# Five places for x instead of three: longer load stretches and whole-slot stores in a store-bound pairwise product kernel

## The chip, the cores and the metric

The kernel runs on one core of one Trainium2 chip. The metric is the device time of one execution in microseconds (us), the median of several executions. "The trace" is one execution taken by the hardware profiler.

## The reference, cut to what matters

```python
def _L0_rec_ref(x, W):                       # x: (4096, 32, 64) f32, W: (64, 64) f32
    vid = jnp.einsum('bfd,de->bfe', x, W)
    idx_i, idx_j = jnp.triu_indices(32, k=1) # 496 pairs of fields, i < j
    return x[:, idx_i, :] * vid[:, idx_j, :] # (4096, 496, 64) f32
```

The input is 33.6 MB and the output 520.1 MB. Almost all of the time goes into writing the output.

## The kernel before: the parts that matter

The batch is cut into 16 tiles of x, each of 128 partitions x 32 fields x 128 numbers, 2.097 MB. TensorE makes `vid` from a tile, in the on-chip memory PSUM. VectorE multiplies x by `vid` for the 496 pairs and writes the products into a slot in the on-chip memory SBUF. A slot goes to DRAM in one or more stores; one pair is 65,536 B. All loads and stores are issued by the SyncE sequencer (SP) on one queue, in the order of the program.

```python
SLOT = 116                                   # pairs in a slot, three slots
GROWING = [45, 46, 25, 55, 61, 44, 72, ...]  # small stores in the first ten slots (cut)
xpool = ctx.enter_context(tc.tile_pool(name="x", bufs=3))
opool = ctx.enter_context(tc.tile_pool(name="out", bufs=3))
...
    load(4)                                  # first tile, in four pieces
    load()
    load()
    for t in range(NT):
        xt = loaded[t]
        ...                                  # 16 matmuls into vid
        for at, m, w, i, di, j, dj in products(blocks(t), t * NP):
            ...                              # one tensor_tensor per block of pairs
            nc.vector.tensor_tensor(o, left, right, ALU.mult)
            at += n
            if at == until or at in (base + SLOT, NT * NP):
                nc.sync.dma_start(out=out[:, sent:at, :], in_=ot[:, sent - base : at - base, :])
                ...
        if t % 2:
            load()
            load()
```

`blocks(t)` takes the pairs of the first two tiles field by field (the first products need few fields) and those of the others in square blocks (fewer, larger operations).

Of the kernel before, what the change touches and what calls it, by code (L numbers as in the profile page):

```python
# [1 line left out]

# [4 lines left out]

F32 = mybir.dt.float32
ALU = mybir.AluOpType

P = 128

C = 128

SLOT = 116

GROWING = [
    45, 46, 25, 55, 61, 44, 72, 58, 58, 77, 39, 87, 29, 76, 40, 90, 26, 33,
    83, 84, 32,
]  # L20

XPAD = 8
OPAD = 24


def by_field():

    return [("row", j, 0, 1, j) for j in range(1, 32)]


def by_block():


    def within(lo):
        yield "step", lo, 2, 1, 0
        for k in range(2):
            yield "step", lo, 4, 2, k
        for i in (lo, lo + 8):
            yield "row", i + 4, i, 4, 4
        yield "row", lo + 8, lo, 8, 8  # L40

    yield from within(0)
    yield "row", 16, 0, 16, 16
    yield from within(16)


def blocks(t):
    return by_field() if t < 2 else by_block()


def products(blocks, at=0):

    for kind, a, b, c, d in blocks:
        if kind == "row":
            rows, n, i0, di, j0, dj = c, d, b, 0, a, 1
        else:
            rows, n, i0, di, j0, dj = 16 // b, c, a, b, a + c + d, b
        r = k = 0
        while r < rows:
            room = SLOT - at % SLOT  # L60
            if k or room < n:
                m, w = 1, min(n - k, room)
            else:
                m, w = min(rows - r, room // n), n
            yield at, m, w, i0 + r * di + k, di, j0 + r * dj, dj
            at += m * w
            if k + w == n:
                r, k = r + m, 0
            else:
                k += w  # L70


def pairs(blocks):

    for _, m, w, i, di, j, dj in products(blocks):
        for r in range(m):
            for k in range(w):
                yield i + r * di + k, j + r * dj


@with_exitstack
def pairwise_bilinear_kernel(
    ctx: ExitStack,
    tc: tile.TileContext,
    x: bass.AP,
    w: bass.AP,
    out: bass.AP,
):




    nc = tc.nc
    NT = x.shape[0]
    F = x.shape[2] - XPAD
    D = P // 2
    NP = F * (F - 1) // 2

    BANK = 512 // C


    ctx.enter_context(tc.manual_schedule(engines={mybir.EngineType.SP}))

    const = ctx.enter_context(tc.tile_pool(name="const", bufs=1))
    xpool = ctx.enter_context(tc.tile_pool(name="x", bufs=3))
    opool = ctx.enter_context(tc.tile_pool(name="out", bufs=3))
    psum = ctx.enter_context(
        tc.tile_pool(name="ps", bufs=1, space=bass.MemoryType.PSUM)
    )
    vid = psum.tile([P, F, C], F32)  # L110


    w2 = const.tile([P, D], F32)
    nc.sync.dma_start(out=w2, in_=w)  # L114

    loaded = []

    def load(pieces=1):
        t = len(loaded)
        if t == NT:  # L120
            return
        xt = xpool.tile([P, F, C], F32, tag="x", name=f"x_{t}")
        n = F // pieces
        for lo in range(0, F, n):
            nc.sync.dma_start(out=xt[:, lo : lo + n, :], in_=x[t][:, lo : lo + n, :])
        loaded.append(xt)

    load(4)
    load()
    load()  # L130

    growing = iter(GROWING)
    until = next(growing)
    sent = 0
    for t in range(NT):
        xt = loaded[t]


        for b in range(0, F, BANK):
            for h in range(2):  # L140
                half = slice(h * D, (h + 1) * D)
                nc.tensor.matmul(  # L142
                    vid[half, b : b + BANK, :],
                    lhsT=w2[half, :],
                    rhs=xt[half, b : b + BANK, :],
                    start=True,
                    stop=True,
                )

        for at, m, w, i, di, j, dj in products(blocks(t), t * NP):  # L150
            base = at - at % SLOT
            if at == base:
                ot = opool.tile([P, SLOT, C], F32, tag="o", name=f"o_{at}")
            n = m * w
            o = ot[:, at - base : at - base + n, :]
            if m == 1:
                left = xt[:, i : i + w, :]
                right = vid[:, j : j + 1, :].to_broadcast([P, w, C])
            else:
                o = o.rearrange("p (m w) c -> p m w c", m=m)  # L160
                right = vid[:, j : j + (m - 1) * dj + 1 : dj, :].unsqueeze(2).to_broadcast([P, m, w, C])
                if di == 0:
                    left = xt[:, i : i + w, :].unsqueeze(1).to_broadcast([P, m, w, C])
                else:
                    left = xt.rearrange("p (m d) c -> p m d c", d=di)[:, i // di : i // di + m, i % di : i % di + w, :]
            nc.vector.tensor_tensor(o, left, right, ALU.mult)  # L166
            at += n
            if at == until or at in (base + SLOT, NT * NP):
                nc.sync.dma_start(
                    out=out[:, sent:at, :],  # L170
                    in_=ot[:, sent - base : at - base, :],
                )
                sent = at
                if at == until:
                    until += next(growing, NT * NP)


        if t % 2:
            load()
            load()  # L180


_INS = ["r_x", "L0_rec_W"]
_OUTS = [((4096, 496, 64), "float32")]


# [37 lines left out]
```

## Time and profile before

| | before |
|---|---|
| time, median | 1292.53 us (3 runs), later 1292.44 (6 runs) |
| span of the profiled execution | 1290.5 us |
| moved through the DMA engines | 553.7 MB, mean 429 GB/s |
| VectorE busy | 1087.0 us, 84% |
| TensorE busy | 219.7 us, 17% |
| loads of x after the head | 13, as six pairs and a single one |

How to read it: the 16 DMA engines are busy in every slice of the span, and VectorE waits for stores, not stores for VectorE. The lines for this are in the prediction below. A word on terms used from here on. A *stretch* is a run of loads with no store between them. A *turn* is the place where the queue goes from stores to loads and back to stores; each stretch has one. The *spread* of a transfer is the time between the first and the last of its 16 landings, one for each DMA engine. From the trace's records of landings I take each transfer's *loss*: the time from the last landing of the transfer before it to its own last landing, less what its bytes need at 435.2 GB/s (the ceiling that the prediction cites).

### The profile page before, as it was taken

The numbers are of one execution on the slowest core, as the hardware profiler recorded it, in microseconds if no ns is written. First come the engines' busy times: TensorE is split into PE (matmuls) and PEld (weight loads), VectorE is DVE, ScalarE is ACT, GpSimd is POOL, SyncE is SP. The second block draws the span as 40 slices with busy tenths as digits, with TensorE's granted clock in tenths as the row PEclk, the third lists the DMA queues.
The fourth block names the chain that finished last, engine by engine and source line by source line (L and its number), as shares of the span: only waits on it lengthen the run. The fifth ranks groups of instructions, "written<-read, shape, count | busy, mean of one in ns | idle before, by whom it ended". The sixth has DMA issues, their size and how long they took to land.

```text
span 1290.5 us, 1722 instructions
## 1 busy us (share of the span) xinstructions
PE 219.7 (17%) x512; PEld 44.3 (3%) x512; DVE 1087.0 (84%) x363; POOL 0.2 (0%) x4
## 2 busy tenths in 40 slices
PE   4121112111121111311123111131101311202000
PEld 1000000000000000000000000000000000000000
DVE  7999989999689886889959989689895998979970
POOL 0000000000000000000000000000000000000000
PEclk8555555555555556555555555555556555555555
DMA  9999999999999999999999999999999999999998
GB/s 390 439 429 436 428 414 434 440 433 431 437 426 434 442 418 442 420 442 438 426 433 425 436 439 421 442 426 436 436 421 438 436 425 439 428 436 436 438 426 350
DMA packets 14265, 553.79 MB, mean 429 GB/s; under 512 B 1712, under 2 KB 1712, under 8 KB 2224
## 3 DMA queue, kind: packets, MB, share of 16 engines
q1 hardware_dynamic: 14256, 553.69, 99.6%
q8 instruction: 4, 0.07, 0.0%
q14 instruction: 5, 0.04, 0.0%
HBM read 33.59 MB, written 520.09 MB: 429 GB/s over the span
## 4 chain that ended last, share of the span: by engine, by line
DMA 62%; DVE 34%; issue 2%; PE 0%; DVEq 0%; SPq 0%
DMA out_dram<-o 61%; DVE o L166 34%; DMA x<-in_r_x_dram 0%; PE vid L142 0%; DVEq L166 0%; SPq L114 0%
## 5 line engine op out<-in xcount | busy, mean ns | idle before, releaser
L166 DVE TENSOR_TENSOR o<-x,vid 128x1024 f32<-128x1024 f32 (+18 forms) x363 | 1087.0, 3064 | 166.5 <-DMA out_dram<-o 156.7
L142 PE MATMUL vid<-x,w 64*64 64x512 f32 x512 | 219.7, 990 | 961.1 <-DVE o L166 755.6
L142 PEld LDWEIGHTS vid<-x,w 64*64 64x64 f32 x512 | 44.3, 199 | 1134.8 <-DVE o L166 871.6
L194 POOL MEMSET const-bfloat16-1.0<- 128x1 bf16 x1 | 0.1, 101 | 0.0
L194 POOL MEMSET const-uint8-127<- 128x1 uint8 x1 | 0.1, 101 | 0.0
L194 POOL MEMSET const-float32-0.0<- 128x1 f32 x1 | 0.1, 98 | 0.2 <-issue 0.2
L194 POOL MEMSET const-float32-1.0<- 128x1 f32 x1 | 0.1, 98 | 0.0
## 6 DMA issues: line engine op xcount, KB each, us to landing
out_dram<-o SPq DMA_DIRECT2D x59, 7424.0 KB, 36.7
x<-in_r_x_dram SPq DMA_DIRECT2D x15, 2048.0 KB, 40.7
out_dram<-o SPq DMA_DIRECT2D x2, 3712.0 KB, 16.7
out_dram<-o SPq DMA_DIRECT2D x1, 5760.0 KB, 22.9
out_dram<-o SPq DMA_DIRECT2D x1, 5568.0 KB, 19.4
out_dram<-o SPq DMA_DIRECT2D x1, 5312.0 KB, 37.0
out_dram<-o SPq DMA_DIRECT2D x1, 4928.0 KB, 17.8
out_dram<-o SPq DMA_DIRECT2D x1, 4864.0 KB, 20.9
```

The lines of the kernel that those rows point to most:

```text
L142: nc.tensor.matmul(vid[half, b : b + BANK, :], lhsT=w2[half, :], rhs=xt[half, b : b + BANK, :], start=True, stop=True,)
L166: nc.vector.tensor_tensor(o, left, right, ALU.mult)
L194: nc = _bacc.Bacc("TRN2", target_bir_lowering=False, num_devices=1, dynamic_dma_scratch_size=1024)
```

## The change

The intent of the change is to turn less often between loads and stores: five places for x allow five tiles at the head and then four loads in one stretch, three times (4, 4 and 3). The longer head also gives VectorE the time to fill a whole slot, so the growing stores and the order by fields can go. Five places take room from the slots, which shrink from 116 to 95 pairs.

```diff
-SLOT = 116
-GROWING = [45, 46, 25, ... ]          (cut)
+SLOT = 95
+PLACES = 5
...
-def by_field(): ...                   (cut)
-def blocks(t):
-    return by_field() if t < 2 else by_block()
...
-    xpool = ctx.enter_context(tc.tile_pool(name="x", bufs=3))
+    xpool = ctx.enter_context(tc.tile_pool(name="x", bufs=PLACES))
...
     load(4)
-    load()
-    load()
+    for _ in range(PLACES - 1):
+        load()
...
-        for at, m, w, i, di, j, dj in products(blocks(t), t * NP):
+        for at, m, w, i, di, j, dj in products(by_block(), t * NP):
...
-            if at == until or at in (base + SLOT, NT * NP):
+            if at in (base + SLOT, NT * NP):
                 nc.sync.dma_start(
-                    out=out[:, sent:at, :],
-                    in_=ot[:, sent - base : at - base, :],
+                    out=out[:, base:at, :], in_=ot[:, : at - base, :]
                 )
...
-        if t % 2:
-            load()
-            load()
+        if (t + 1) % (PLACES - 1) == 0:
+            for _ in range(PLACES - 1):
+                load()
```

More of the change, by code (lines that the diff above doesn't have):

```diff
@@ L13 @@
 C = 128
-SLOT = 116
-GROWING = [
-    45, 46, 25, 55, 61, 44, 72, 58, 58, 77, 39, 87, 29, 76, 40, 90, 26, 33,
-    83, 84, 32,
-]
+SLOT = 95
+PLACES = 5
 XPAD = 8
 OPAD = 24
-def by_field():
-    return [("row", j, 0, 1, j) for j in range(1, 32)]
 def by_block():
@@ L128, in pairwise_bilinear_kernel @@
     load(4)
-    load()
-    load()
-    growing = iter(GROWING)
-    until = next(growing)
-    sent = 0
+    for _ in range(PLACES - 1):
+        load()
     for t in range(NT):
@@ L167, in pairwise_bilinear_kernel @@
             at += n
-            if at == until or at in (base + SLOT, NT * NP):
+            if at in (base + SLOT, NT * NP):
                 nc.sync.dma_start(
-                    out=out[:, sent:at, :],
-                    in_=ot[:, sent - base : at - base, :],
-                )
-                sent = at
-                if at == until:
-                    until += next(growing, NT * NP)
-        if t % 2:
-            load()
-            load()
+                    out=out[:, base:at, :], in_=ot[:, : at - base, :]
+                )
+        if (t + 1) % (PLACES - 1) == 0:
+            for _ in range(PLACES - 1):
+                load()
 _INS = ["r_x", "L0_rec_W"]
@@ L220 @@
     for t in range(NT):
-        order = [place[p] for p in pairs(blocks(t))]
+        order = [place[p] for p in pairs(by_block())]
         res[:, t][:, :, order] = got[:, :, t].transpose(0, 3, 2, 1)
```

## The prediction

> **What bounds the kernel now.** I read the page first (slices, bytes, the chain's shares), then the groups, then the chain in order of time, then busy times by stretches for both ends. The page:
>
> ```profile
> DMA  9999999999999999999999999999999999999998
> GB/s 390 439 429 436 428 414 434 440 433 431 437 426 434 442 418 442 420 442 438 426 433 425 436 439 421 442 426 436 436 421 438 436 425 439 428 436 436 438 426 350
> HBM read 33.59 MB, written 520.09 MB: 429 GB/s over the span
> DMA 62%; DVE 34%; issue 2%; PE 0%; DVEq 0%; SPq 0%
> ```
>
> The DMA engines are busy in every slice. Bytes are fixed: 16 tiles of x of 2.097 MB in, 7936 pairs of 65,536 B out. The multiplies are the only other large row:
>
> ```profile
> L166 DVE TENSOR_TENSOR o<-x,vid 128x1024 f32<-128x1024 f32 (+18 forms) x363 | 1087.0, 3064 | 166.5 <-DMA out_dram<-o 156.7
> ```
>
> VectorE is busy 84% of the span and idles mainly for a free slot, that is for a store. So it is ahead, and its time only matters where it might leave the queue empty. The chain in order of time (start, duration, what), where the end of each DMA piece is the landing of a store:
>
> ```profile
> 257.78 36.65 DMA out_dram<-o
> ...
> 310.63 46.65 DMA out_dram<-o
> ...
> 425.67 37.14 DMA out_dram<-o
> ...
> 478.75 47.36 DMA out_dram<-o
> ...
> 1047.40 36.59 DMA out_dram<-o
> ...
> 1100.06 41.35 DMA out_dram<-o
> ...
> 1157.24 36.69 DMA out_dram<-o
> ```
>
> These landings lie three slots apart. From 1141.41 (1100.06 + 41.35) to 1193.93 is 52.52 us for 3 x 116 x 65,536 B = 22.81 MB: 434 GB/s, the rate with stores alone. From 294.43 to 357.28 is 62.85, and from 462.81 to 526.11 is 63.30: a pair of loads between the stores costs 10.35 and 10.8 us, where its 4.19 MB at 434 GB/s need 9.66. From 1083.99 to 1141.41 is 57.42: the one load at the end costs 4.90 against 4.83. So a pair loses 0.7 to 1.1 us, a single load almost nothing.
>
> What that is I looked up in the trace's own records, each DMA's 16 landings and each packet. Five full pairs from the second on lose about 0.6, 1.1, 1.0, 0.9 and 0.9 us, nearly all in the pair's **last** load (the first loses 0.00 to 0.07); the pair at 141 us loses 2.6. In the pair that lands at 654 and 659 us every load packet takes 0.61 us, on into the second load, until other engines begin to store; then some twenty packets take 0.7 to 1.6 us. The loss thus sits at the turn from loads to stores, on the engines still loading. The 16 landings of one transfer spread 1.1 us at the head, 5.3 us at the end: the laggards set the time.
>
> The ends:
>
> ```profile
> 0.00:10.00 10.00, 4.46 (x12) 1.55 (x14) 1.82 (x5) 0.20 (x4) 1.00 0.79 300
> 10.00:20.00 10.00, 8.20 (x36) 2.38 (x32) 10.00 (x9) 0.00 (x0) 1.00 1.03 439
> 1270.00:1280.00 10.00, 0.00 (x0) 0.00 (x0) 0.00 (x0) 0.00 (x0) 0.50 0.94 406
> 1280.00:1290.50 10.50, 0.00 (x0) 0.00 (x0) 0.00 (x0) 0.00 (x0) 0.50 0.43 185
> ```
>
> The last column is GB/s. The first 10 us lose (434 - 300) x 10 = 1.34 MB, 3.1 us; from 10 us on the rate is full, so the growing small stores already hide the head.
>
> Budget: 553.7 MB at 434.4 GB/s is 1274.6 us; the span is 1290.5. Of the 15.9 us between, the start takes 3 to 4, load turns some 7 (2.6 + 4.5 + 0.1), the last receipts and the rest of the spread 4 to 5.
>
> **What the Trainium skill says.** "DMA: Bandwidth & Descriptors", section "Where 436 GB/s comes from", gives a ceiling of 435.2 GB/s at the SBUF ports: stores here run at 434, within 0.3%, so no slot size can speed a store up. The same page, "Rules for kernel authors", asks for at least 1 MiB per DMA; all whole slots and tiles, before and after, exceed that. "VectorE: DVE Perf Modes", section "The TRN2 errata", gives (N+151)/0.96 ns for an fp32 add of two tensors: 1224 ns at N = 1024. With one operand in PSUM the groups here show 1215 (1024), 8681 (8192) and 12948 (12288), which is (N+142)/0.96; I use that. I know no sentence there on a cost of turning from loads to stores; that rests on this trace alone.
>
> **The change, part by part.**
> 1. *Head.* Five tiles are loaded before the first store, not three: the same bytes, moved forward. Nothing is saved if the first store stands in the queue before the loads are through. The third tile landed at 19.25 us; two more at 5.0 each land at 29.2, first engines at about 28, and their data end about a microsecond earlier: the store must be issued by some 25.7 if it needs the 1.3 us that the first small load needed before data flowed. The block order starts with 8 pairs that need fields 0 to 15, thus four PSUM banks: the last matmul of bank 3 ends at 12.0 (11.39 + 0.59). Slot 0 is seven operations: 3 x 1.215 + 2 x 2.281 + 4.415 + 1.081 = 13.7 us, so the store is issued at 25.7. Just in time: 0, at worst some half us of gap. After that a slot takes 13.0 to 14.0 us to multiply (95 x 128 x 1.0417 ns = 12.67, plus 2 to 9 operations at 0.148) against 95 x 65,536 B at 434.4 GB/s = 14.33 us to store: VectorE gains about a microsecond per slot and the queue never runs dry.
> 2. *By fields to by blocks, smaller slots.* Operations go from 363 to 415 by count of the two programs: 52 x 0.148 = 7.7 us at most, all of it under VectorE's 166 us of idle time: 0 on the path.
> 3. *Stores.* 84 in place of 79. Each store's landing falls about 0.04 us behind the pure rate whatever its size: +0.2 us.
> 4. *Load stretches.* Before: six pairs and a single load after the head. After: 4, 4 and 3. If the loss is at the turn, three turns at 1.1 us plus 0.05 for each of the other eight loads make 3.7; before it was 7.4 in all. Saved: 3.7 us.
> 5. *Room.* Four tiles hold the queue for 4 x 2.097 MB / 434.4 GB/s = 19.3 us, while VectorE fills the slots left and then idles some 20 us. When the first store after the stretch lands, two full slots wait in the queue, 28.7 us of work; less the spread of 6 us, 22 remain for a fill of 13 to 14. No gap. The fourth load waits for its tile's last multiply, 84, 73 or 62 pairs into a slot, at most 12 us after the third is issued, with two stores and three loads queued ahead of it: hidden as well. PE refills vid in 8 us under the 17 us of a tile's first half.
>
> Sum: 1292.53 + 0.2 + 0 to 0.5 - 3.7 = 1289.1 or so; I say 1289.0.
>
> **The rivals.**
> *A: the loss is per load that follows a load.* Then 6 such loads before become 3 + 3 + 2 = 8, and the time stays at 1292.5 to 1294. For it: the second of each pair has the loss and the single last load has none. Against it: the packets are slow only from the moment other engines store, not from the start of the second load.
> *B: a hole in the queue.* With slots 18% smaller, the queue holds less; if a stretch, or the fourth load's wait which also holds back the store behind it, empties the queue by 3 us three times, the time is about 1298. Against: 22 us of stock for 14 of work. For: the spread could grow.
> *C: turns cost nothing like the single load's 0.1 and the spread stays small.* Then all 7 us are won: 1285.5. Against: five pairs of six lost 0.6 to 1.1.
> *D: the extra loads at the head delay everything.* 4.19 MB, 9.7 us, if VectorE were the bound; but the queue is busy throughout, so only the order changes.
>
> **Range and chances.** I give the turn theory about 0.7, A 0.15, B 0.07, C 0.08. The turns vary from 0.1 to 2.6 us each, so three of them spread the result by about 2 us either way: 1286.3 to 1292.4. Two per cent is 25.8 us; all the loss that isn't plain rate is 15.9, so faster by 2% is as good as excluded. Slower by 2% needs a queue empty for 26 us, for which nothing speaks.
>
> **What would show it.** In the chain, landings three slots apart should be 43.0 us without loads (18.68 MB) and 63 to 64 with four (43.0 + 19.3 + 1.1): under 63 is C, about 65.5 is A. VectorE's wait for stores should show three long waits of about 20 us, its operations 415. The first slice should read as before, with the first store issued at 25 to 26 us. DMA must be 9 in every slice; an 8 in a slice with loads is B. I am wrong if the spread grows as much with three stretches as with seven, or if the store rate itself shifts from 434 GB/s with the 48,640 B rows.

## The result, and the profile after

The changed kernel takes 1291.01 us in the median (1290.52 to 1291.07, six runs), the kernel before beside it 1292.44 (1292.04 to 1292.58). The ratio is 0.9989, with a 95% interval from 0.9976 to 1.0002. A second set of five runs (e9 below) gave 1290.57 against 1292.41, ratio 0.9987, interval 0.9973 to 1.0000. Ratios are the mean time of one kernel's fast runs over that of the other's fast runs of the same rounds, so they are not quite the ratio of the medians. At 2% the two are the same. The gain is 1.4 to 1.8 us, seen twice with the same sign, but each interval alone still reaches 1. Run by run it is clearer: all 11 runs of the changed kernel (1290.12 to 1291.28) are faster than every run of the kernel before (1291.34 and up).

The page of the changed kernel, busy share of DMA and GB/s in 40 slices, the bytes, the chain's shares and the VectorE row:

```profile
DMA  9999999999999999999999999999999999999998
GB/s 397 435 435 433 433 435 435 432 435 413 432 435 435 435 431 433 432 435 435 419 427 435 435 435 434 435 433 433 433 422 425 433 435 435 434 435 435 435 435 362
HBM read 33.59 MB, written 520.09 MB: 430 GB/s over the span
DMA 58%; DVE 34%; another core or an unknown queue 4%; DVEq 1%; issue 1%; PE 0%; SPq 0%
L151 DVE TENSOR_TENSOR o<-x,vid 128x1024 f32<-128x1024 f32 (+17 forms) x415 | 1092.0, 2698 | 166.2 <-DMA out_dram<-o 155.0
```

The queue never runs dry. There are 415 multiplies as counted, VectorE's 1092 us are 5 more than before and its idle time is the same 166 us, so nothing on VectorE shows in the time. In the GB/s row the three stretches can be seen in the slices with 413, with 419 and 427, and with 422 and 425; elsewhere, but for the two ends, the row stands at 431 to 435.

The waits of the changed kernel (in total, how often, longest): the longest wait of VectorE for a store is now 22.6 us, the first stretch of four loads seen from VectorE. The other two stretches give 22.0 and 17.6, so there are the three long waits that the prediction named.

```profile
DVE o L151 <- DMA out_dram<-o: 155.0, 76, 22.6
```

The chain in order of time (start, duration, what). A piece ends with the landing of a store; the piece called an unknown queue ends, by its time, with a store's landing too.

```profile
287.13 29.79 DMA out_dram<-o
...
330.03 22.52 another core or an unknown queue
...
394.54 29.78 DMA out_dram<-o
...
437.39 29.96 DMA out_dram<-o
...
610.64 29.70 DMA out_dram<-o
...
653.38 21.88 another core or an unknown queue
```

From 424.32 (394.54 + 29.78) to 467.35 lie three slots without loads: 43.03 us for 18.68 MB, again 434 GB/s, so the smaller rows haven't changed the store rate. From 316.92 to 352.55 lie one slot and four loads: 35.63 us, where 6.23 MB and 8.39 MB at 434 GB/s need 33.66. This turn loses 2.0 us. The next one, from 640.34 to 675.26, loses 1.3.

The ends and the first turn in stretches (the last three columns are the granted clock, DMA share and GB/s):

```profile
0.00:10.00 10.00, 4.50 (x12) 1.53 (x14) 0.00 (x0) 0.20 (x4) 1.00 0.81 308
10.00:20.00 10.00, 6.72 (x30) 1.75 (x26) 8.83 (x6) 0.00 (x0) 0.99 1.00 429
20.00:30.00 10.00, 3.94 (x8) 0.59 (x8) 10.00 (x5) 0.00 (x0) 0.50 1.09 451
...
318.00:332.00 14.00, 5.85 (x16) 1.79 (x16) 12.03 (x3) 0.00 (x0) 0.62 1.01 432
332.00:335.00 3.00, 0.00 (x0) 0.00 (x0) 0.00 (x0) 0.00 (x0) 0.50 1.04 328
1270.00:1280.00 10.00, 0.00 (x0) 0.00 (x0) 0.00 (x0) 0.00 (x0) 0.50 0.98 424
1280.00:1290.00 10.00, 0.00 (x0) 0.00 (x0) 0.00 (x0) 0.00 (x0) 0.50 0.41 178
```

The head shows no hole: 429 and 451 GB/s from 10 to 30 us. In the stretch the loads run at 432 GB/s until the last three microseconds before the stores begin, and there at 328 with the engines just as busy. The records of packets say the same in single transfers. From 318 to 332 us a load packet takes 0.61 us; of the 38 that start from 333 to 335 us, 32 take 0.7 to 1.4 us; the first packet of the next store starts at 335.5. At the other side of the stretch the last store packets before the loads take up to 2.63 us (at 313 us) where 1.80 is usual. So a turn costs at both of its sides, and the slow load packets come before the stores begin, not beside them. The prediction read this otherwise ("until other engines begin to store"); but in the pair it names, too, 11 of the 22 slow load packets start before the first store packet, which starts at 655.00 us.

Where the time went, from the landings of both traces, in us. "Loads after the head" counts the stores on both sides of each stretch too. "Jumps" are single store landings away from any load that lose more than 0.15 us at once (up to 1.0 here).

| loss against 435.2 GB/s | before | changed | e9 (changed again) |
|---|---|---|---|
| start, head loads and first store | 4.8 | 5.2 | 5.1 |
| loads after the head, with the stores on both sides | 7.9 | 5.3 | 4.7 |
| jumps | 2.2 | 1.9 | 1.7 |
| all other stores | 2.4 | 2.8 | 3.4 |
| sum at the last landing | 17.3 | 15.3 | 14.9 |
| spread of the last store | 6.1 | 3.9 | 3.6 |
| average landing of the last store, us | 1285.5 | 1284.9 | 1284.8 |

The last two rows were the surprise. The average engine finishes only 0.5 us earlier in the changed kernel. The slowest engine, which sets the time, finishes 2.0 us earlier. Three quarters of the gain is thus a smaller lag of the slowest engine behind the average. Within a turn the average is hit as well: of the 5.3 us of the three stretches the average of the 16 landings loses 4.4.

### The profile page after: what moved, and what is told of

The parts are those of the page before. It is cut to its first block, busy times and chain, and to the rows that moved or that the text cites. A ratio compares the mean times of both kernels' runs of the same rounds, so it can differ in the third digit from the quotient of the medians.

```text
span 1288.7 us, 1786 instructions
## 1 busy us (share of the span) xinstructions
PE 226.6 (18%) x512; PEld 41.9 (3%) x512; DVE 1092.0 (85%) x415; POOL 0.2 (0%) x4
## 4 chain that ended last, share of the span: by engine, by line
DMA 58%; DVE 34%; another core or an unknown queue 4%; DVEq 1%; issue 1%; PE 0%; SPq 0%
DMA out_dram<-o 58%; DVE o L151 34%; DVEq L193 1%; PE vid L127 0%; DMA x<-in_r_x_dram 0%; DVEq L151 0%; SPq L102 0%
## 5 line engine op out<-in xcount | busy, mean ns | idle before, releaser
L151 DVE TENSOR_TENSOR o<-x,vid 128x1024 f32<-128x1024 f32 (+17 forms) x415 | 1092.0, 2698 | 166.2 <-DMA out_dram<-o 155.0
L127 PE MATMUL vid<-x,w 64*64 64x512 f32 x512 | 226.6, 1008 | 959.0 <-DVE o L151 892.6
```

The source lines that it names most:

```text
L127: nc.tensor.matmul(vid[half, b : b + BANK, :], lhsT=w2[half, :], rhs=xt[half, b : b + BANK, :], start=True, stop=True,)
```

## The experiments

The theory after the result: each turn makes the late engines later, by about a microsecond, whatever the length of the stretch, so that the time depends on the number of turns (turn theory). Rivals: the loss goes with the loads that follow another load (length theory); a turn costs more while all engines turn together (spread theory). Each experiment is an edit of the changed kernel. All but e4 gave correct results. The kernel before, run beside them on the same chip, had medians of 1292.36 (e1 to e4), 1292.32 (e5 to e8) and 1292.41 (e9, e10).

**e1: pairs of loads**

```diff
-        if (t + 1) % (PLACES - 1) == 0:
-            for _ in range(PLACES - 1):
+        if (t + 1) % 2 == 0:
+            for _ in range(2):
                 load()
```

> The changed kernel, but its 11 later loads go two after every second tile (2,2,2,2,2,1) in place of 4,4,3; head, slots and stores as in the changed kernel. In the changed kernel's trace the three stretches cost 2.0, 1.3 and 1.8 us over their bytes (5.2 in all), not the 3.7 predicted. Turn theory (each turn from loads to stores costs about 1.2 us, whatever the length of the stretch): six turns, about 7 us, so +2 us on the changed kernel, 1292.5 to 1293.5. Length theory (the loss grows with the loads that follow a load: 5 here against 8): 3 us, so 1289. Spread theory (a turn costs more while all engines turn together): between, falling from turn to turn.

Measured: 1293.16 us (1292.54 to 1293.35), ratio to before 1.0004 (0.9990 to 1.0018). This is 2.2 us above the changed kernel and inside the range of the turn theory. The length theory said 1289. No run of it is as fast as any run of the changed kernel. Loads after the head lose 8.3 us, against 5.3. It also says something of the rest of the change: with six turns to the seven of before, the kernel is not faster than before, so the other parts together (order of the blocks, whole slots, slot size, head) gain nothing, and the longer stretches make the gain.

**e2: single loads**

```diff
-        if (t + 1) % (PLACES - 1) == 0:
-            for _ in range(PLACES - 1):
-                load()
+        load()
```

> The changed kernel, but one load after every tile (eleven stretches of one). Turn theory: eleven turns at about 1.2 us make 13 against 5.2, so about 1299. Length theory (a load alone costs only its bytes, as the single one at the end of the kernel before did, 0.1 us): 1 us against 5.2, so about 1287, which would beat both kernels. Each load should show in the trace as 4.83 us plus its loss.

Measured: 1298.68 us (1296.58 to 1299.46), ratio 1.0045 (1.0032 to 1.0058). The turn theory gave 1299, the length theory 1287. Loads lose 15.8 us in all, 1.4 for each turn. The single load at the end of the kernel before, which cost 0.1, was thus not typical of single loads. The turns also grow dearer as the spread grows: the first five lose 0.4 to 1.3 us, with a spread of up to 4 us in the store before them, the last five 1.8 to 2.0, with 7 to 13 us. That is the opposite of the spread theory. The landings of the last store show where it goes: its average is 1285.9, only 1.0 us later than in the changed kernel, while its last engine is 9.0 us later. The spread has grown to 13.0 us.

**e3: three tiles at the head**

```diff
     load(4)
-    for _ in range(PLACES - 1):
+    for _ in range(2):
         load()
 ...
                 nc.sync.dma_start(out=out[:, base:at, :], in_=ot[:, : at - base, :])
+                if base == 0:
+                    load()
+                    load()
```

> The changed kernel, but only three tiles are loaded at the head, the other two right behind the first store. The first store is issued at about 24.4 us as before, while three tiles are through at about 18. If the five tiles at the head are what fills the time until the first whole slot, the DMA engines stand still for 24.4 + 1.3 - 18 = 7 to 8 us and the time is about 1298.5. If the head doesn't matter because the order of the same bytes is all that changes, it stays at 1291. It also adds one turn (1 us).

Measured: 1299.12 us (1298.16 to 1299.73), ratio 1.0050 (1.0036 to 1.0064), as the head theory expected. Busy time by stretches of this run, to be set against the same two stretches of the changed kernel above (429 and 451 GB/s):

```profile
10.00:20.00 10.00, 7.54 (x30) 1.89 (x26) 8.01 (x6) 0.00 (x0) 1.00 0.76 326
20.00:30.00 10.00, 3.26 (x8) 0.58 (x8) 10.00 (x5) 0.00 (x0) 0.58 0.55 233
```

The DMA engines stand still between the third tile and the first whole slot, while VectorE is busy (10.00 of 10 us in the second line). The first store lands with a loss of 8.9 us. So five tiles at the head do fill the time that the growing stores filled before. (The run also has one turn more than the changed kernel.)

**e4: no loads after the head (wrong result)**

```diff
-        xt = loaded[t]
+        xt = loaded[t % PLACES]
 ...
-        if (t + 1) % (PLACES - 1) == 0:
-            for _ in range(PLACES - 1):
-                load()
```

> WRONG RESULT ON PURPOSE: the changed kernel without the 11 later loads (tiles 5 to 15 multiply the first five again), so the queue holds nothing but stores after the head. 23.07 MB less at 434.4 GB/s are 53.1 us. If the turns cost what the trace shows (5.2 us) the time is 1291.0 - 53.1 - 5.2 = 1232.7. If the stretches cost only their bytes, 1237.9. The spread of the landings should stay near 1.3 us except for the jumps of about 1 us on a store that both traces show (before at 462.8, 863.4 and 1264.8 us, after at 145.1 and 482.6); if those come with the loads, they are gone.

Measured: 1233.98 us (1233.81 to 1234.17). The changed kernel's 1291.01 less this is 57.0 us for 23.07 MB of loads; their bytes need 53.1, so three turns cost 3.9 us, 1.3 each. That is less than the 5.3 of the landings, since this run's own stores lose more (4.2 us in plain stores and 2.7 in jumps, against 2.8 and 1.9). The spread of the last store is 1.7 us: without turns it hardly grows from the 1.1 of the head. The jumps, however, are still there, so they do not come from the loads. The page's bytes and the chain around the largest one (start, duration, what):

```profile
HBM read 10.52 MB, written 520.09 MB: 431 GB/s over the span
```

```profile
387.48 29.59 DMA out_dram<-o
...
430.14 31.32 DMA out_dram<-o
...
474.53 29.92 DMA out_dram<-o
```

From 417.07 to 461.46 are 44.39 us for three slots, from 461.46 to 504.45 are 42.99: a jump of 1.4 us with nothing but stores in the queue. What lies there is in the packet records: a packet of the instruction queue, 16 KB, starts at 443.5 us and takes 0.95 us, and a store packet that starts just as it ends, at 444.5, takes 2.18 us where 1.80 is usual. 0.95 + 0.38 is 1.3 us, the jump. In the page these packets are two small rows under the queues (here those of the changed kernel: packets, MB, share of the engines):

```profile
q1 hardware_dynamic: 14976, 553.69, 99.7%
q8 instruction: 4, 0.07, 0.0%
q14 instruction: 6, 0.05, 0.0%
```

The two jumps in the changed kernel (landings at 145.1 and 482.6 us) and the three in the kernel before (462.8, 863.4 and 1264.8) each follow a packet of one of these two rows by 2 to 15 us, less than the 30 us that a store takes from issue to landing. All eight jumps of e6 below follow one by 2.7 to 5.7 us, all four of e7 by 2.9 to 3.0. Most of these packets show no jump: the changed kernel has nine between 140 us and the end of its data, and two jumps. It fits that a fetch takes time on one DMA engine, and delays the end only where that engine is a late one. This is read from the order of the records; no run took the fetches away.

**e5: six places, two turns**

```diff
-SLOT = 95
-PLACES = 5
+SLOT = 84
+PLACES = 6
```

> The changed kernel with six places for x in slots of 84 pairs: six tiles at the head, then 5 and 5, so two turns in place of three. By the runs so far a turn is worth about 1.0 us (0, 3, 6 and 11 turns: 1287.1 after adding the bytes of the loads, 1291.0, 1293.2, 1298.7) to 1.7 us (the stretches in the changed kernel's trace). Stores: 95 in place of 84, 0.5 us at 0.045 each. Turn theory: 1290.0 to 1290.5, faster than both kernels. Length theory (already weak): a stretch of five costs more than one of four and nothing is won, 1291 to 1292.

Measured: 1291.07 us (1290.71 to 1291.75), ratio 0.9990 (0.9977 to 1.0002): a miss, no faster than the changed kernel. The loads lose 3.5 us in two stretches, against 5.3 in three, so a turn costs 1.7 us here, about as in the changed kernel (1.8). The other stores lose 3.7 against 2.8 us, and the jumps 3.0 against 1.9, with one of 1.5 us; the head loses 0.5 us more, as its last tile lands 1.0 us late. What one turn less gave was eaten by the stores, the jumps and the head.

**e6: nine places, one turn**

```diff
-SLOT = 95
-PLACES = 5
+SLOT = 52
+PLACES = 9
```

> Nine places for x in slots of 52 pairs: nine tiles at the head, then one stretch of seven, so one turn. Two turns less are worth 2 to 3.4 us, but 153 stores in place of 84 cost 69 x 0.045 = 3.1 us if the loss of 0.045 us is per store whatever its size. Then 1291 to 1292. If that loss goes with the bytes and not with the stores, about 1288.5. If the queue runs empty with three small slots (two of them hold 15.7 us, a fill takes 7.2), well over 1293.

Measured: 1294.14 us (1294.02 to 1294.28), ratio 1.0013 (0.9999 to 1.0026), 2 us above the range of the per-store theory. The loads lose 2.6 us, 2.7 less than in the changed kernel. The other stores lose 6.0 us, 3.2 more, which is 0.046 for each of the 69 added and as expected. The missing part is jumps: eight of them, 5.5 us against 1.9.

**e7: every slot as two stores**

```diff
-                nc.sync.dma_start(
-                    out=out[:, base:at, :], in_=ot[:, : at - base, :]
-                )
+                half = (at - base) // 2
+                for lo, hi in ((0, half), (half, at - base)):
+                    nc.sync.dma_start(
+                        out=out[:, base + lo : base + hi, :], in_=ot[:, lo:hi, :]
+                    )
```

> The changed kernel, but every slot goes out as two stores (47 and 48 pairs), both issued when the slot is full: 168 stores, everything else as in the changed kernel. Per-store theory: 84 x 0.045 = 3.8 us, so 1294.8. If the shortfall against 435.2 GB/s goes with the bytes, 1291.0. The turns stay three.

Measured: 1296.93 us (1296.84 to 1297.59), ratio 1.0035 (1.0021 to 1.0049): 5.9 us over the changed kernel, more than the per-store theory's 3.8 and far from none. By the landings, plain stores lose 6.5 us against 2.8, so 0.04 for each added store, as expected. The rest is 1.5 us in the turns (6.8 against 5.3) and 1.4 in jumps (3.3 against 1.9). In the DMA issues of this run the two rows of 83 show the same bytes in twice the stores:

```profile
out_dram<-o SPq DMA_DIRECT2D x83, 3072.0 KB, 30.0
out_dram<-o SPq DMA_DIRECT2D x83, 3008.0 KB, 24.9
```

**e8: later loads on the second queue**

```diff
-    ctx.enter_context(tc.manual_schedule(engines={mybir.EngineType.SP}))
+    ctx.enter_context(tc.manual_schedule(engines={mybir.EngineType.SP, mybir.EngineType.Activation}))
 ...
-            nc.sync.dma_start(out=xt[:, lo : lo + n, :], in_=x[t][:, lo : lo + n, :])
+            (nc.sync if t < PLACES else nc.scalar).dma_start(out=xt[:, lo : lo + n, :], in_=x[t][:, lo : lo + n, :])
```

> The changed kernel, but the 11 later loads are issued by ScalarE's sequencer, on the second queue, so that each engine can alternate between a load and a store packet, and no load waits behind the stores in SP's order. If every change of direction on an engine costs what a turn costs (some 1.4 us of engine time for the two changes), eight load packets per engine and load, 11 loads, make up to 88 changes and the time goes far up, over 1310. If the loss comes only once per stretch, when all engines change together, mixing would cost less: 1287 to 1291.

Measured: 1296.84 us (1295.10 to 1297.03), ratio 1.0030 (1.0017 to 1.0044), between the two expectations: no cost at every packet, and no gain over the changed kernel. The queues of this run show the loads moved:

```profile
q1 hardware_dynamic: 13392, 530.62, 95.2%
q10 hardware_dynamic: 1584, 23.07, 4.2%
```

The edit has a side effect. On their own sequencer the loads are no longer held back by SP's order and go one by one, as soon as a tile is done (the first at 79 us in place of 288), so this is nearer to e2 than to the changed kernel. It is 1.8 us below e2's 1298.68, but the intervals of the two ratios overlap and the order of the transfers differs, so what mixing is worth stays open. The average engine's last landing is 1286.7 us, 1.8 later than in the changed kernel, the spread 11.0 us.

**e9: the changed kernel again.** No edit.

> The changed kernel once more, unchanged, for more rounds beside the kernel before: its first interval, 0.9976 to 1.0002, just includes 1. If the gain of 1.4 us is real, 1290.5 to 1291.2 again, beside 1292.0 to 1292.6. If it was chance, no difference.

Measured: 1290.57 us (1290.12 to 1291.28), ratio 0.9987 (0.9973 to 1.0000). The trace repeats the first one closely: the jumps stand at 144.8 and 482.3 us again, and the loads lose 4.7 us.

**e10: four places, four turns**

```diff
-SLOT = 95
-PLACES = 5
+SLOT = 105
+PLACES = 4
```

> Four places for x in slots of 105 pairs: four tiles at the head, then four stretches of three, so four turns and 76 stores. Turn theory: one turn more than the changed kernel is worth 1.0 to 1.3 us, eight stores fewer at 0.04 give 0.3 us back: 1291.7 to 1292.0. Length theory (already weak): 8 loads that follow a load, as in the changed kernel, so 1291.0 or below.

Measured: 1295.29 us (1294.41 to 1295.73), ratio 1.0021 (1.0008 to 1.0033): 3.4 us above the turn theory's range. What I overlooked was the head. Four tiles are through at 23.7 us, but the first slot of 105 pairs is only stored from 26.2 us on. Busy time by stretches of this run:

```profile
20.00:30.00 10.00, 3.60 (x8) 0.58 (x8) 10.00 (x5) 0.00 (x0) 0.55 0.66 283
```

283 GB/s is the hole; the first store's landing loses 4.0 us. Without these 4.0 the time would be 1291.3 by my estimate, below the turn theory's 1291.7, so this run does not separate the theories. It does show that head and slot have to be sized together: the loads must last as long as the first slot takes to fill.

The runs with 95-pair slots sent whole, sorted by turns after the head:

| turns | run | time, us | loss on loads, us | spread of the last store, us | its average landing, us |
|---|---|---|---|---|---|
| 0 | e4 | 1233.98 + 53.1 for the bytes left out = 1287.1 | 0 | 1.7 | 1230.3 + 53.1 = 1283.4 |
| 3 | changed, e9 | 1291.01, 1290.57 | 5.3, 4.7 | 3.9, 3.6 | 1284.9, 1284.8 |
| 6 | e1 | 1293.16 | 8.3 | 6.8 | 1285.0 |
| 11 | e2 | 1298.68 | 15.8 | 13.0 | 1285.9 |

From none to eleven turns the time rises by 11.6 us, 1.05 for each. In the traced executions the average landing of the last store gives 2.5 of them; the lag of the last engine behind the average grows by 9.5 (from 1.0 to 10.6). Within the turns the average loses 4.4 us in the changed kernel, 5.0 in e1 and 6.1 in e2, so the further turns fall almost wholly on the late engines, but the three stretches do not.

## Why the prediction was right or wrong, point by point

The prediction said 1289.0, with a range of 1286.3 to 1292.4, and no difference of 2%. The time of 1291.0 lies in the range, in its upper half. The gain of 1.4 us (1.8 in e9) is about half of the predicted 3.5. The mechanism, that the loss goes with the turns and not with the loads, was right; one term of the sum was mis-sized.

1. *Head.* Right. The first store was issued at 24.41 us, before the 25.7 of the working, and there is no hole. e3 shows what the two extra tiles are worth (8 us, with one more turn). The "0 to half a us" is there as 0.4 us (5.2 against 4.8 in the table), but it isn't a gap: it is the turn at the end of the head, where the fifth tile's landing loses 0.6 us. So it came to the predicted size by luck.
2. *VectorE.* Right: 415 operations, 5 us more busy time, none of it on the path.
3. *Stores.* The 0.04 us per store was right in plain running; e7 and e6 give 0.04. For 84 stores in place of 79 that is the predicted 0.2; the table's row shows 0.4 us more. That row has 75 stores against 61, since fewer stand beside a turn, so even 0.6 would be expected.
4. *Load stretches.* This is the step that was mis-sized: "three turns at 1.1 us plus 0.05 for each of the other eight loads make 3.7". The 1.1 held: the last loads of the three stretches lost 1.2, 1.1 and 1.2 us (e9: 0.9, 0.8, 0.9). The 0.05 failed for the first load of a stretch, at the side from stores to loads: these lost 0.6, 0.05 and 0.4 us (e9: 1.0, 0.05, 0.3). The loads alone lost 4.9 us (e9: 4.2) in place of 3.7, and before 7.3 in place of 7.4, so 2.4 us were saved (e9: 3.1) and not 3.7. The prediction had taken the first loads from the pairs after the first one (0.00 to 0.07) and left the 0.55 of the first pair out. The spread theory does not explain the size, since e2 goes against it. By length of the stretch, with the stores on both sides, a turn costs 1.4 us for single loads (e2) and pairs (e1; 1.1 in the kernel before), 1.6 to 1.8 for three to five loads (e10, e9, changed, e5) and 2.6 for the one stretch of seven (e6). It thus grows a little with length, but slot size and head differ too in e10, e5 and e6; why it grows is not shown.
5. *Room.* Right: DMA reads 9 in every slice but the last, as before.

Of the rivals, A (loss per load that follows a load) is refuted by e1 and e2, which move opposite to it. It would have given 65.5 us for three slots and four loads, the turn theory 63.4; the chain gives 64.3 at 316.92 (two more slots at 14.34 added to the 35.63) and 63.6 at 640.34. B (a hole in the queue) did not come. C (turns as cheap as the single load) is refuted by e2, where single loads cost 1.4 us each. D did not come.

The prediction saw the second half of the mechanism ("the laggards set the time") but did not put it into its sum, where a turn is lost throughput alone. The runs show that further turns push mostly the late engines back: from three turns to eleven the average's loss in the turns goes from 4.4 to 6.1 us, that of the last landings from 5.3 to 15.8. Why packets slow down just before the change of direction, and why late engines stay late, the records do not show: they name neither the engine of a packet nor what it waits for. That stays open.

No variant beat the changed kernel. Fewer turns need more places for x, which make smaller slots and more stores (e5, e6); larger slots need more turns or open a hole at the head (e10). Five places with 95 pairs are the best that was tried, level with six places and 84 pairs.

## What to carry to other kernels

When one DMA queue carries both directions and is busy throughout, count how often it turns: here each turn was worth about 1 us at the end (1.1 to 2.6 us by its own landings, the most for the longest stretch), and splitting stores cost about 0.04 us each plus more at the turns and in jumps. Look at the 16 landings of a transfer one by one, since the time is that of the latest engine and the mean rate does not show it. Size the head loads and the first store together, so that the loads end no earlier than the first slot is full.

## What the Trainium skill lacked or had wrong

- "DMA: Bandwidth & Descriptors", section "Bandwidth": it gives the ceiling (435.2 GB/s; the stores here ran at 434) but says nothing of turns between loads and stores on one queue. Here 0, 3, 6 and 11 turns made 1287.1 (with the bytes left out added), 1291.0, 1293.2 and 1298.7 us.
- The same page, section "Anatomy of one DMA": its fixed cost of about 2.0 us per DMA, for DMAs issued from gpsimd, is put down mainly to completion latency. The page has no figure for what a further DMA costs in a full queue. Here 84 further stores of the same bytes cost 5.9 us, 0.07 each (e7).
- The same page, section "Why a DMA increments its semaphore by 16 and not by 1", says that a DMA's engines finish independently. It does not say that spread adds up over a kernel (1.7 us without turns, 13.0 with eleven).
- The same page, section "Issuing engines are not separate DMA queues", says that DMAs issued from several engines run on the same 16 DMA engines and interleave. It does not say what interleaving loads with stores costs or gains; e8 took 1296.8 us against 1291.0, but its loads also went in another order.
- No page says that an instruction fetch can hold up data. Here a packet of 0.95 us stood before a jump of 1.4 us (e4).
- "VectorE: DVE Perf Modes", section on the TRN2 errata: (N+151)/0.96 ns for an fp32 add of two tensors; the page has no such formula with one operand in PSUM, where the product here took (N+142)/0.96, 1215 ns at N = 1024.
